# A feed-forward block on one core: another head and one more slot by seven products

## The chip, the core and the metric

The program runs on one core of one Trainium2 chip. TensorE (PE in the profile) does the matmuls, VectorE (DVE), ScalarE (ACT) and GpSimd (POOL) do the work on whole tiles, SyncE (SP) issues most of the DMAs. The metric is the device time of one execution in microseconds (us).

## What is computed

`x` is 4 batches of 1024 tokens of 512 numbers. The reference, cut to what matters:

```python
scale = cond @ norm_w.T + 1.0                       # (4, 512)
h = x * (scale[:, None, :] * rsqrt(mean(x * x) + EPS))
val, gate = split(h @ up_w.T, 2)                    # up_w: 4096 x 512
h = val * gelu(gate)                                # 2048 wide
hq = act_quant(h)                                   # 8 bit, one scale for each token
y = hq @ weight_quant(down_w).T + x                 # down_w: three values
```

## The kernel before, in words

The 2048 columns of `h` are made in 16 slots of 128 columns (`NJ`) for each batch, so there are 64 slots; slot g of batch 0 has the weights W_g, with 128 value rows and 128 gate rows. Each number of `x` and of W is split into two fp16 parts, high and low, and of the four products of parts three are taken, so a product of 128 x 256 by 256 x 512 is six matmuls (`TERMS`).

In batch 0 the slots below `SEVEN` are taken plainly: `plain_half(j, h)` runs 24 matmuls for each half of the tokens, 48 for a slot. From slot `SEVEN` on, and in all later batches, `slot(g)` takes seven products of sums and differences of blocks (A, B, E are its PSUM banks), 42 matmuls for a slot. What these seven products need of the weights is made by `s_sums`, `s_high`, `s_low` and stored with `s_spill`; what they need of `x` in batch 0 is made by the steps in `FIRST_T`. A slot at or above `SEVEN` gets its sums turned by one DMA transpose at once, and later batches load it as it is; one below has them turned at each later load (`s_load_x`, `s_load_y`).

The head is the part before the first product. SyncE loads `x` and W0 to W2. TensorE runs 23 idle matmuls (`keep_warm`), and among them the three small steps of the condition: `cond_first_row` (pc, line 685) spreads the condition's row over the partitions, VectorE forms the scale of batch 0 (`cond_scale`, `cond_largest`), TensorE turns the largest (line 715), VectorE makes a power of two of it (`cond_range`), TensorE spreads it (line 731). `first_sum` sums the squares of the first four tiles of `x`, `rsqrt` is an affine step and a power (POOL, lines 1001 and 1002) and gives `rs0`. `first_scale` multiplies each tile with its `rs0`, `first_turn` transposes the tile on TensorE. `w_range(j)` finds the largest of the weights' rows on VectorE (line 786) and their inverse `iv` (line 796); `w_scale(j)` multiplies them with it; `w_turn(j)` transposes them on TensorE (line 825); `w_high` and `w_low` copy the high part out of PSUM and subtract it for the low one (lines 850 to 862). `first_high` (ACT, line 1498) and `first_low` (DVE, line 1502) do the same for `x`. Then `plain_first` runs slot 0 for the first half of the tokens (24 matmuls, line 1199), in an order written by hand into which the turns of W1 and W2 are set.

Nothing of this is issued in the order of the code. All steps are recorded in a `Plan`; a planner places them by estimated durations and due times, `MENDS` is a list of random seeds by which it mends the waits that it foresees, `MOVES` is a list of pairs (step, step before which it is put), and what comes out is the order on each engine. Every engine then runs its own row in order and waits on semaphores.

Of the kernel before, what the change touches and what calls it, by code (L numbers as in the profile page):

```python
# [115 lines left out]
class Plan:  # L116
# [71 lines left out]

    def order(self):

        steps = self.steps
# [12 lines left out]
        self.lucks = [[(chance.random(), chance.random()) for _ in steps] for _ in range(MISSES)]  # L204
        for n in range(ROUNDS):
            margin, guard, chained, crowded = MARGINS[n % len(MARGINS)]
            self.needed(clock, chained)
            if crowded:
                self.crowd()
            for s in steps:  # L210
                s.margin, s.guard = margin, guard
            order, kept = self.placed()
            clock = self.replay(order)
        for n in MENDS:
            order, kept = self.mend(order, kept, random.Random(n))
        return self.moved(order)

    def moved(self, order):
# [12 lines left out]
        self.replay([s for row in rows.values() for s in row])  # L231
        return sorted(self.steps, key=lambda s: (s.start, s.n))

    def placed(self):
# [5 lines left out]
    def mend(self, order, kept, chance):  # L240
# [5 lines left out]
        for s in order:  # L246
            if s.eng == "PE":
                if s.start - last > 0.08:
                    waits.append((s.start - last, s))
                last = s.end  # L250
        s = chance.choices([s for _, s in waits], [w for w, _ in waits])[0]
        chain, swap, q = [], None, s.behind
        while q is not None and q.eng != "PE" and len(chain) < 20:
            chain.append(q)
            p = q.queue or q.behind
            if p is not None and p.n not in q.deps and chance.random() < 0.5:
                swap = chance.random() < 0.6 and p.eng != "PE" and p.late < q.late
                break
            q = p
        if swap:  # L260
            p.late, q.late = q.late + 2e-3, p.late - 2e-3
        elif chance.random() < 0.3 or not chain:
            t, late = s.start, [s.late for s in steps]
            self.needed(clock, chance.random() < 0.5)
            margin, guard, _, _ = chance.choice(MARGINS)
            for s, old in zip(steps, late):
                if s.tied or not t - 50.0 < s.late < t + 5.0:
                    s.late = old
                    continue
                s.margin, s.guard = margin, guard  # L270
                if s.eng != "PE":
                    s.late -= chance.random() ** 4
        else:
            sooner = 0.2 + 8.0 * chance.random() ** 2
# [77 lines left out]
    def replay(self, order, luck=None):  # L352
# [9 lines left out]
        while True:  # L362
# [19 lines left out]
            s, t = first[1], first[2]  # L382
            cost = s.alone
            if luck and s.eng != "PE":
                cost *= 0.96 + 0.12 * luck[s.n][0]
            if s.port:
                if port > t + 0.1:
                    s.behind = holder
# [4 lines left out]
            if s.wait:  # L393
                x, s.queue = t + ISSUE, None
                if s.wait > 0.1:
                    if dma > x:
                        x, s.queue = dma, last
                    dma, last = x + s.wait, s
                s.end = x + s.wait + LANDING + (luck[s.n][1] if luck else 0.0)
            if s.end > latest:  # L400
                latest = s.end

# [11 lines left out]
)  # L414
CROWD, ROOM = (45.0, 215.0), 1.05
MOVES = (
# [7 lines left out]
)  # L424
ROUNDS = 1
MENDS = (
# [7 lines left out]
)  # L434
MISSES, ISSUE, LANDING, RELOAD, FETCH, FERRY = 6, 1.2, 1.5, 6.5, 8.6, 4.0


# [113 lines left out]
def glu_quant_kernel(  # L551
# [246 lines left out]
    def w_range(j, t0=0, t1=2):  # L798
        w_factor(j, w_largest(j, t0, t1), t0, t1)
# [5 lines left out]

    ROWS = 3

    SEVEN = 9

    def w_scale(j, ts=(1, 0), eng=None):  # L810
        eng = eng or (ACT if j >= 5 else POOL)
# [684 lines left out]
    def first_high(h, k, pt):  # L1496
        c = slice(h * TOK, (h + 1) * TOK)
        ACT.activation(XP[:, 0, k, c], pt, AF.Copy, scale=scT[:, k, 0:1])

    def first_low(h, k, pt, eng=DVE):  # L1500
        c = slice(h * TOK, (h + 1) * TOK)
# [29 lines left out]
    first_sum(1)  # L1531
    first_sum(2)
    first_sum(3, DVE)
    w_range(0, 1, 2)
    rsqrt(ssq0[:, 0:4], rs0[:, 0:4])
    first_scale(2, DVE)
    first_scale(0, ACT)
    first_scale(1, POOL)
    first_scale(3, ACT)
    w_scale(0, (1,))  # L1540
    ptx = [po_bank(f"ptx_0_{k}") for k in range(3)] + [bank("A", 2, name="ptx_0_3")]
    for n in (2, 0, 1, 3):
        first_turn(n, ptx)
    book.tied = False
    w_turn(0, [bank("E", 2, name=f"pw_0_{t}") for t in (1, 0)], (1,))
# [560 lines left out]
```

## Time and profile before

| what | us |
|---|---|
| median of 3 runs (719.23 to 719.73) | 719.45 |
| the profiled execution | 719.23 |
| its span, from the first to the last instruction | 717.4 |
| TensorE busy in the span | 711.5 |
| VectorE / ScalarE / GpSimd busy | 605.2 / 409.8 / 130.0 |
| first matmul of slot 0 (line 1199) | 14.36 |
| first matmul of a slot by seven products (line 1141) | 112.20 |

The profiled execution's 719.23 is its span and 1.8 us around it. Times inside the program are counted from the start of the span. A line of the timeline has the start, the time taken, the engine, the line of the kernel, the operation, what it writes and reads with the shapes, how many instructions are merged in it, and in brackets the idle time of the engine before it with what ended it. TensorE's matmuls overlap in the records: one of 512 columns is shown with 0.38 us, but the next starts after 0.216.

### The profile page before, as it was taken

The page shows a single profiled execution, that of the slowest core. Times are in us where ns is not written, and L with a number is a line of the kernel's source. Part 1 is how long each engine was busy: PE and PEld are TensorE (multiplying, and loading weights), DVE is VectorE, ACT ScalarE, POOL GpSimd, SP SyncE. Part 2 cuts the span into 40 slices and gives each one's busy share as a digit, 9 for nine tenths or more (in the row PEclk, how much of TensorE's full clock was granted, in tenths as well). Part 3 has the DMA queues.
Part 4 walks back from the last instruction along what each step waited for, and adds up shares of the span by engine and source line. Part 5 has one row for each costly group of instructions (what it writes and reads, how often), then busy time and mean ns, then how long its engine had stood idle before and what let it go on. Part 6 is the DMA issues. An engine that isn't in the chain of part 4 may idle for free.

```text
span 717.4 us, 10113 instructions
## 1 busy us (share of the span) xinstructions
PE 711.5 (99%) x3625; PEld 355.8 (50%) x3625; DVE 605.2 (84%) x903; ACT 409.8 (57%) x671; POOL 130.0 (18%) x138
## 2 busy tenths in 40 slices
PE   8999999999999999999999999999999999999998
PEld 4544444444444456664444445665444444445744
DVE  7978998899899899878899887767878888956897
ACT  5677688784546897553435786533333775332454
POOL 4753141020100004660023003700011000000000
PEclk9999999999999999999999999999999999999999
DMA  7778999999785896759234555778233444453414
GB/s 261 253 205 208 240 227 252 194 257 268 219 227 133 210 245 173 223 153 211 67 101 110 118 129 142 176 191 173 73 118 103 102 102 99 99 98 104 150 57 146
DMA packets 189134, 118.74 MB, mean 166 GB/s; under 512 B 151302, under 2 KB 158359, under 8 KB 189084
## 3 DMA queue, kind: packets, MB, share of 16 engines
q1 hardware_dynamic: 188794, 117.77, 64.3%
q8 instruction: 28, 0.46, 0.3%
q10 hardware_dynamic: 290, 0.33, 0.1%
q14 instruction: 22, 0.18, 0.1%
HBM read 59.20 MB, written 23.09 MB: 115 GB/s over the span
## 4 chain that ended last, share of the span: by engine, by line
PE 97%; DMA 1%; ACT 1%; POOL 0%; DVE 0%; issue 0%; SPq 0%; POOLq 0%
PE A L1141 40%; PE E L1141 20%; PE B L1141 10%; PE po L1413 9%; PE E L1156 6%; PE A L1156 4%; PE B L1156 3%; PE po L1362 2%; PE E L1362 1%; PE A L1362 1%; DMA H<-in_x_dram 1%; PE B L1413 1%; PE B L1362 0%; PE A L1199 0%; PE po L1494 0%; PE po L825 0%
## 5 line engine op out<-in xcount | busy, mean ns | idle before, releaser
L1141 PEld LDWEIGHTS <-SXY 128*128 128x128 f16 x2184 | 213.7, 98 | 250.9
L1141 PE MATMUL A<-R,SXY 128*128 128x512 f16 x1188 | 276.3, 379 | 0.0
L1141 PE MATMUL E<-R,SXY 128*128 128x512 f16 x594 | 145.3, 379 | 0.0
L1334 DVE TENSOR_TENSOR H<-H,am 128x1024 f32<-128x1024 f32 x64 | 76.6, 1222 | 0.2
L1141 PE MATMUL B<-R,SXY 128*128 128x512 f16 x312 | 76.6, 379 | 0.0
L1275 DVE TENSOR_REDUCE gm<-H 128x512 f32<-128x1024 f32 x56 | 69.0, 1232 | 0.9
L1252 ACT ACTIVATE t<-t,sg 128x512 f32<-128x512 f32 x55 | 39.7, 721 | 51.0 <-DVE t L1249 51.0
L1239 DVE SCALAR_TENSOR_TENSOR H<-A,sg,t 128x512 f32<-128x512 f32 x55 | 41.2, 749 | 31.9 <-PE A L1141 31.6
L1291 POOL PARTITION_ALL_REDUCE am<-R x8 | 15.5, 1934 | 288.4 <-DVE R L1277 288.4
L1236 ACT ACTIVATE t<-B,sg 128x512 f32<-128x512 f32 x55 | 37.8, 687 | 42.7 <-PE B L1141 42.6
L1227 ACT COPY B<-A 128x512 f32<-128x512 f32 x55 | 31.4, 571 | 53.3 <-PE A L1141 53.1
L1249 DVE TENSOR_TENSOR t<-E,t 128x512 f32<-128x512 f32 x55 | 37.9, 689 | 28.2 <-PE E L1141 27.7
L1413 PE MATMUL po<-wd,R 128*128 128x256 fp8e4 (+1 forms) x448 | 57.0, 275 | 0.0
L1219 ACT COPY t<-A 128x512 f32<-128x512 f32 x55 | 32.2, 585 | 43.4 <-PE A L1141 39.0
L1255 DVE TENSOR_TENSOR v<-A,v 128x512 f32<-128x512 f32 x55 | 37.9, 690 | 20.4 <-PE A L1141 19.6
L1413 PEld LDWEIGHTS <-R 128*128 128x128 bf16 (+1 forms) x480 | 47.0, 98 | 13.1
L1231 ACT COPY v<-E 128x512 f32<-128x512 f32 x55 | 32.2, 586 | 31.9 <-PE E L1141 15.6
L1342 ACT ACTIVATE H<-H 128x1024 f32<-128x1024 f32 x38 | 39.7, 1049 | 8.5 <-DVE H L1334 8.3
L1258 DVE SCALAR_TENSOR_TENSOR H<-v,sg,t 128x512 f32<-128x512 f32 x55 | 41.7, 759 | 1.7 <-ACT t L1252 1.4
L1156 PEld LDWEIGHTS <-SXY 128*128 128x128 f16 x264 | 25.8, 98 | 30.5
L1346 ACT ACTIVATE R<-H 128x1024 bf16<-128x1024 f32 x38 | 39.6, 1052 | 1.0 <-DVE H L1086 0.5
L1277 DVE TENSOR_TENSOR R<-R,gm 128x512 f32<-128x512 f32 x56 | 38.4, 686 | 0.9
(270 smaller groups left out, 919.2 us busy)
## 6 DMA issues: line engine op xcount, KB each, us to landing
SXY<-s_dram SPq DMA_DIRECT2D x57, 256.0 KB, 2.7
H<-in_L_cond_up_w_dram SPq DMA_DIRECT2D x13, 512.0 KB, 4.1
SXY<-s_dram SPq DMA_DIRECT2D x15, 384.0 KB, 3.7
xr<-in_x_dram SPq DMA_DIRECT2D x19, 256.0 KB, 2.9
out_dram<-xr SPq DMA_DIRECT2D x19, 256.0 KB, 2.1
s_dram<-SXY SPq DMA_DIRECT2D x12, 384.0 KB, 3.6
s_dram<-SXY SPq DMA_DIRECT2D x5, 896.0 KB, 6.7
H<-in_x_dram SPq DMA_DIRECT2D x8, 512.0 KB, 4.8
```

The source lines that it names most:

```text
L1141: PE.matmul(o, s[:, w, k, :], xs(l, k), start=start and n == 0, stop=stop and n == len(TERMS) - 1, skip_group_check=True,)
L1156: PE.matmul(ps, a[k // 2][:, w, k % 2, :], XP[:, l, k, h * TOK : (h + 1) * TOK], start=n == 0, stop=n == len(terms) - 1,)
L1239: DVE.scalar_tensor_tensor(h_half(g - 1, 0), prev["A"], gain(g - 1, 0), prev["t1"], ALU.mult, ALU.mult)
L1249: DVE.tensor_tensor(prev["t2"], prev["E"], prev["t2"], ALU.add)
L1252: ACT.activation(prev["t2"], prev["t2"], AF.Gelu, scale=gain(g - 1, 1))
L1258: DVE.scalar_tensor_tensor(h_half(g - 1, 1), prev["v"], gain(g - 1, 0), prev["t2"], ALU.mult, ALU.mult)
L1275: DVE.tensor_reduce(gm[0], v, AX.X, ALU.max, apply_absolute_value=True)
L1277: return [largest, lambda: DVE.tensor_tensor(m, m, gm[0], ALU.max)]
L1334: DVE.tensor_tensor(v, v, r.to_broadcast([P, 2, TOK]), ALU.mult)
L1342: ACT.activation(v, v, AF.Copy, bias=MAGIC)
L1346: ACT.activation(q, by_tile(v), AF.Copy, bias=-MAGIC)
L1413: PE.matmul(po, w[:, j], m, start=start and j == 0, stop=stop and j == n - 1, skip_group_check=True,)
```

## The change

What the code does now, in the head and in slot 8:

```diff
-    SEVEN = 9
+    SEVEN = 8
...
     first_sum(3, DVE)
+    rsqrt(ssq0[:, 0:4], rs0[:, 0:4], DVE)
     w_range(0, 1, 2)
-    rsqrt(ssq0[:, 0:4], rs0[:, 0:4])
+    w_scale(0, (1,), ACT)
+    first_scale(0, DVE)
     first_scale(2, DVE)
-    first_scale(0, ACT)
-    first_scale(1, POOL)
-    first_scale(3, ACT)
-    w_scale(0, (1,))
+    first_scale(1, ACT)
+    first_scale(3, DVE)
...
-    for n in (2, 0, 1, 3):
+    for n in (0, 2, 1, 3):
         first_turn(n, ptx)
```

The affine step of `rsqrt` goes from GpSimd to VectorE (the power stays on GpSimd), three tiles of `x` are scaled on VectorE and one on ScalarE, and the gate rows of W0 on ScalarE in place of GpSimd. Slot 8 is taken by seven products. `first_high` gets an engine argument, which no call uses; `begin` does nothing with the empty `HEAD`.

The planner's tables are all new, so that the order on every engine differs from before in many places. `MOVES` has 288 pairs in place of 46, `MENDS` 68 other seeds, `mend` looks only at the first `REACH` matmuls (160, 400, 800 or 4000 of them in turn):

```diff
-    (1063, 1016), (56, 76), (96, 132), (2119, 2167), (98, 94), (1064, 1016), (307, 275), (295, 31),
+    (5604, 5615), (5603, 5614), (5602, 5611), (5601, 5602), (5598, 5601), (5608, 5596), (3183,
...
+        for s in [s for s in order if s.eng == "PE"][:reach]:
+            if s.start - last > 0.08:
+                waits.append((s.start - last, s))
+            last = s.end
```

Three places of the new order are shown, by the rows of one engine. Line numbers of the kernel after the change are 52 to 55 higher here: 1565 is 1510 (the idle matmuls), 737 is 685 (pc), 767 is 715, 877 is 825 (turns of weights), 1251 is 1199 (slot 0).

The first place is TensorE's row from its beginning, before the change: pc is its fourth matmul, behind three idle ones.

```order
L1510 LDWEIGHTS H
L1510 MATMUL A_89<-H 128x512
L685 MATMUL B_90<-H,one 128x128
L1510 LDWEIGHTS H
L1510 MATMUL A_91<-H 128x512
```

After the change the same stretch reads as follows, and ahead of it stand nine more idle matmuls.

```order
L1565 LDWEIGHTS H
L1565 MATMUL A_91<-H 128x512
L737 MATMUL B_90<-H,one 128x128
L767 MATMUL A_89<-ident,mx_92 1x128
L1565 LDWEIGHTS H
```

So pc is now TensorE's eleventh matmul, behind ten idle ones, and the turn of the largest follows it directly.

The second place is VectorE's row from the condition's power of two on (d, dg), before: `ux`, `dx`, the sum of squares of tile 3, the largest of W0's gate rows, one tile scaled, then the inverses and W0's turned gate rows (CAST).

```order
L725 TENSOR_SCALAR dg_94<-ident,d_0_93 1x1
L735 RECIPROCAL ux<-B_90 128x1
L738 COPY dx<-B_90 128x1
L1482 SCALAR_TENSOR_TENSOR R,ssq_0_87<-H 128x512
L786 TENSOR_REDUCE wam_95<-H 128x1
L659 TENSOR_SCALAR wam_95<-wam_95 128x1
L793 TENSOR_SCALAR sw<-wam_95 128x1
L1489 TENSOR_SCALAR H<-H,rs_0_88 128x512
L796 RECIPROCAL iv_96<-sw 128x1
L786 TENSOR_REDUCE wam_102<-H 128x1
```

After, from the sum of squares on, the rows to the CAST are these.

```order
L1541 TENSOR_SCALAR H<-H,rs_0_88 128x512 x3
L845 TENSOR_SCALAR sw<-wam_95 128x1
L838 TENSOR_REDUCE wam_102<-H 128x1
L848 RECIPROCAL iv_96<-sw 128x1
L711 TENSOR_SCALAR wam_102<-wam_102 128x1
L845 TENSOR_SCALAR sw<-wam_102 128x1
L789 TENSOR_SCALAR scT<-scT,ux 128x4
L848 RECIPROCAL iv_96<-sw 128x1
L838 TENSOR_REDUCE wam_95<-H 128x2
L711 TENSOR_SCALAR wam_95<-wam_95 128x2
L902 CAST SXY<-E_100 128x2x256
```

Ahead of these stand `dg`, the sum of squares, `dx`, the affine step on `ssq`, `ux` and the largest of W0's gate rows, in this order. The three scalings now stand ahead of both inverses of W0 (`iv`), and the largest of both halves of W1 (128x2) ahead of the CAST.

The third place is GpSimd's row and TensorE's at the turns of W1. GpSimd's row after the change, from the power on: the scaling of W0's value rows, the four sums of slot 0 (lines 919 to 922), the scaling of W1's value rows (`iv_103`).

```order
L1054 TENSOR_TENSOR rs_0_88<-ssq_0_87,neghalf 128x4
L869 TENSOR_SCALAR H<-H,iv_96 128x512
L919 TENSOR_TENSOR H<-H 128x256
L921 TENSOR_TENSOR H<-H 128x256
L922 TENSOR_TENSOR H<-H 128x256
L920 TENSOR_TENSOR H<-H 128x256
L869 TENSOR_SCALAR H<-H,iv_103 128x512
```

Before, the sums of slot 0 stood ahead of that scaling too, and the low parts of three of them (line 884) as well. TensorE's row before, where slot 0's first 17 matmuls end and W1 is turned (gate rows into po_97, value rows into po_98):

```order
L1199 LDWEIGHTS SXY
L1199 MATMUL A_89<-R,SXY 128x512
L825 MATMUL po_97<-ident,H 128x128 x4
L825 MATMUL po_98<-ident,H 128x128 x4
L1199 LDWEIGHTS SXY
```

After, the turn of W1's value rows stands here:

```order
L877 MATMUL E_101<-ident,H 128x128 x4
L1251 LDWEIGHTS SXY
L1251 MATMUL B_90<-R,SXY 128x512
L1251 LDWEIGHTS SXY
L1251 MATMUL A_89<-R,SXY 128x512
L1251 LDWEIGHTS SXY
L1251 MATMUL A_89<-R,SXY 128x512
L1251 LDWEIGHTS SXY
L1251 MATMUL B_90<-R,SXY 128x512
L877 MATMUL po_98<-ident,H 128x128 x4
```

So four matmuls of slot 0 stand ahead of it in place of 17. All 24 transposes of the first four tiles of `x` and of W0 stand ahead of slot 0 in both.

More of the change, by code (lines that the diff above doesn't have):

```diff
@@ L189, in order @@
     def order(self):
+        self.begin(HEAD)
         steps = self.steps
@@ L214, in order @@
         for n in MENDS:
-            order, kept = self.mend(order, kept, random.Random(n))
+            order, kept = self.mend(order, kept, random.Random(n), REACH[n % len(REACH)])
         return self.moved(order)
@@ L232, in moved, with begin @@
         return sorted(self.steps, key=lambda s: (s.start, s.n))
+    def begin(self, head):
+        if not head:
+            return
+        first, last, new = set(head), {}, {}
+        self.steps = [self.steps[n] for n in head] + [s for s in self.steps if s.n not in first]
+        for n, s in enumerate(self.steps):
+            new[s.n], s.n = n, n
+        for s in self.steps:
+            s.deps = {new[d] for d in s.deps}
+        for s in self.steps[: len(head)]:
+            if s.wait:
+                continue
+            if s.eng in last:
+                s.deps.add(last[s.eng])
+            last[s.eng], s.tied = s.n, True
     def placed(self):
@@ L238, in placed, with mend @@
         return sorted(self.steps, key=lambda s: (s.start, s.n)), kept
-    def mend(self, order, kept, chance):
+    def mend(self, order, kept, chance, reach):
         steps, last, waits = self.steps, 0.0, []
@@ L245, in mend @@
         clock = self.replay(order, chance.choice(self.lucks))
[L246 to L250, printed above, removed]
+        for s in [s for s in order if s.eng == "PE"][:reach]:
+            if s.start - last > 0.08:
+                waits.append((s.start - last, s))
+            last = s.end
         s = chance.choices([s for _, s in waits], [w for w, _ in waits])[0]
@@ L384, in replay @@
             if luck and s.eng != "PE":
-                cost *= 0.96 + 0.12 * luck[s.n][0]
+                cost *= 0.97 + 0.09 * luck[s.n][0]
             if s.port:
@@ L398, in replay @@
                     dma, last = x + s.wait, s
-                s.end = x + s.wait + LANDING + (luck[s.n][1] if luck else 0.0)
+                s.end = x + s.wait + LANDING + (0.7 * luck[s.n][1] if luck else 0.0)
             if s.end > latest:
@@ L426 @@
 MENDS = (
[7 rows of a table removed]
-)
[9 rows of a table added]
+)
+REACH = (160, 400, 800, 4000)
+HEAD = ()
 MISSES, ISSUE, LANDING, RELOAD, FETCH, FERRY = 6, 1.2, 1.5, 6.5, 8.6, 4.0
@@ L1494, in first_turn, with first_high @@
             PE.transpose(pts[k][:, c : c + P], X0[:, n, k * P : (k + 1) * P], ident)
-    def first_high(h, k, pt):
+    def first_high(h, k, pt, eng=ACT):
         c = slice(h * TOK, (h + 1) * TOK)
-        ACT.activation(XP[:, 0, k, c], pt, AF.Copy, scale=scT[:, k, 0:1])
+        if eng is ACT:
+            ACT.activation(XP[:, 0, k, c], pt, AF.Copy, scale=scT[:, k, 0:1])
+        else:
+            eng.tensor_scalar(XP[:, 0, k, c], pt, scT[:, k, 0:1], None, ALU.mult)
     def first_low(h, k, pt, eng=DVE):
```

59 rows, old and new, of tables (MENDS, MOVES) are left out of this document.

## The prediction

> **What bounds the kernel now.** I read the page first (busy times), then the busy times by stage, then the chain that ended last, then the first 45 us row by row. On the page TensorE is busy for nearly the whole span.
>
> ```profile
> span 717.4 us, 10113 instructions
> PE 711.5 (99%) x3625; PEld 355.8 (50%) x3625; DVE 605.2 (84%) x903; ACT 409.8 (57%) x671; POOL 130.0 (18%) x138
> ```
>
> The table by stage says where the rest is (columns: stretch, its length, busy time and instructions of PE, PEld, DVE, ACT, POOL, clock, DMA share, GB/s). From 20 us on PE is busy all the time, at the full granted clock; VectorE is at 9.97 of 10 in one stage, and the DMA engines are full around 100 us.
>
> ```profile
> 30.00:40.00 10.00, 10.00 (x56) 5.38 (x54) 9.97 (x19) 6.24 (x13) 6.66 (x9) 1.00 0.80 266
> 100.00:125.00 25.00, 25.00 (x118) 11.33 (x116) 22.07 (x43) 22.68 (x40) 3.56 (x4) 1.00 1.06 251
> 250.00:700.00 450.00, 450.00 (x2386) 233.26 (x2384) 370.48 (x482) 232.33 (x369) 71.17 (x73) 1.00 0.53 133
> ```
>
> The chain that ended last gives the price of a matmul and the start of slot 9.
>
> ```profile
> 39.43 2.59 PE A L1156 x12
> 112.36 3.45 PE A L1141 x16
> ```
>
> Twelve take 2.59 us, so one is 0.216. TensorE never catches up after 20 us: a microsecond that its products start later is a microsecond of the end, and a matmul less is 0.216 less. So the sum is short: matmuls removed, and the shift of the moment from which TensorE runs through.
>
> **Slot 8.** 48 matmuls become 42: 6 x 0.216 = **1.30 us less**. What it costs stands beside TensorE: three more copies on ScalarE and two more additions on VectorE, priced by the rows of the later slots (0.57 and 0.69 us), one more DMA transpose at once and six fewer in later batches.
>
> ```profile
> L1227 ACT COPY B<-A 128x512 f32<-128x512 f32 x55 | 31.4, 571 | 53.3 <-PE A L1141 53.1
> L1249 DVE TENSOR_TENSOR t<-E,t 128x512 f32<-128x512 f32 x55 | 37.9, 689 | 28.2 <-PE E L1141 27.7
> ```
>
> That is 1.7 us of ScalarE and 1.4 of VectorE in a stage in which each has 2 to 3 us idle of 25. I cost them at nothing; the cover is that idle time. If it is gone, each piece that is late costs its own length, 0.6 to 1.2 us. More delicate is that the sums of `x` and the turned weights are due 10.4 us sooner, at 102 us in place of 112; that is a rival below.
>
> **The condition behind ten idle matmuls.** These rows carry the head up to the power.
>
> ```profile
> 0.93 0.27 DVE L605 MEMSET H<- 128x256 uint32 x1
> 1.26 1.46 PE L1510 MATMUL A<-H 128*128 128x512 f16 x3 [1.26 <-DVE H L607]
> 2.65 0.79 PE L685 MATMUL B<-H,one 1*128 1x128 f32 x2
> 3.37 2.31 PE L1510 MATMUL A<-H 128*128 128x512 f16 x5
> 3.59 0.29 DVE L690 SCALAR_TENSOR_TENSOR R<-R,B 128x128 f32<-128x128 f32 x1
> 5.12 0.16 DVE L708 TENSOR_REDUCE mx<-scT 128x1 f32<-128x4 f32 x1
> 5.48 0.42 PE L715 MATMUL A<-ident,mx 128*1 128x128 f32 x1
> 5.94 0.28 DVE L721 TENSOR_REDUCE d<-A 1x1 f32<-1x128 f32 x1 [0.66 <-PE A L715]
> 6.60 0.20 DVE L725 TENSOR_SCALAR dg<-ident,d 1x1 f32<-1x1 f32 x1
> 7.17 2.98 PE L1510 MATMUL A<-H 128*128 128x512 f16 x13
> 7.76 0.69 DVE L1482 SCALAR_TENSOR_TENSOR R<-H 128x512 f32<-128x512 f32 x1 [0.26 <-DMA H<-in_x_dram]
> 8.37 0.08 DVE L1482 DVE_READ_ACCUMULATOR R<-H 128x1 f32 x1
> 9.04 1.06 POOL L1002 TENSOR_TENSOR rs<-ssq,neghalf 128x4 f32<-128x4 f32 x1
> ```
>
> The five idle matmuls from 3.37 reach to 5.48: 0.42 each, half the later pace. The warming memset now comes first on VectorE, where three short memsets stood ahead of it, so TensorE starts some 0.1 sooner, at 1.1. Ten at 0.42 put pc at 5.3, where it stood at 2.65. VectorE starts 0.94 after pc, at 6.25 if pc runs at the slow pace throughout, at 5.9 if the pace doubles under it; I take 6.1, since the slow pace is seen until 5.48. To the end of `mx` 1.69 pass (3.59 to 5.28), to line 721 another 0.66, of which some 0.2 was a wait behind idle matmuls, to the end of `dg` 0.86 (5.94 to 6.80). So `dg` ends at 6.1 + 1.69 + 0.5 + 0.86 = 9.15. The sum of squares of tile 3 stands behind it on VectorE: 9.1 in place of 7.76, where the DMA was last. It and its read take 0.69, to 9.8; `dx` and the affine step some 0.25; the step to GpSimd 0.1, the power 1.06: `rs0` at 11.15, the first scaling at **11.2** in place of 10.14. Bounds: 10.7 (faster idle matmuls, no waits between) and 11.5 (slow pace to the end of pc, 0.66 kept).
>
> The Trainium skill, "TensorE: Matmul & The Clock Gate", section "What's actually happening", says that the array runs at half its clock until one busy window of about 3.4 us, and that the window runs free of the kernel's start. The trace agrees (0.42 before 5.48, 0.216 later); by the earliest window, 4.5 us as an estimate of that page, pc would come 0.4 us sooner and the sum 0.4 lower.
>
> **From the scalings to the turn of W1.** Let T be the first scaling on VectorE. Before:
>
> ```profile
> 10.14 0.49 DVE L1489 TENSOR_SCALAR H<-H,rs 128x512 f32<-128x512 f32 x1 [0.66 <-POOL rs L1002]
> 10.54 0.16 DVE L796 RECIPROCAL iv<-sw 128x1 f32<-128x1 f32 x1
> 10.61 0.67 DVE L786 TENSOR_REDUCE wam<-H 128x1 f32<-128x512 f32 x1
> 11.31 0.15 DVE L659 TENSOR_SCALAR wam<-wam 128x1 int32<-128x1 int32 x1
> 11.79 0.15 DVE L796 RECIPROCAL iv<-sw 128x1 f32<-128x1 f32 x1
> 12.03 0.70 POOL L817 TENSOR_SCALAR H<-H,iv 128x512 f32<-128x512 f32 x1 [0.17 <-DVE iv L796]
> 12.81 0.73 POOL L867 TENSOR_TENSOR H<-H 128x256 f32<-128x256 f32 x1
> 13.50 0.73 POOL L868 TENSOR_TENSOR H<-H 128x256 f32<-128x256 f32 x1
> 14.19 0.72 POOL L869 TENSOR_TENSOR H<-H 128x256 f32<-128x256 f32 x1
> 14.36 2.10 PE L1199 MATMUL B<-R,SXY 128*128 128x512 f16 x9 [0.37 <-ACT R L1498]
> 14.99 0.73 POOL L870 TENSOR_TENSOR H<-H 128x256 f32<-128x256 f32 x1
> 16.52 1.90 PE L1199 MATMUL A<-R,SXY 128*128 128x512 f16 x8
> 17.89 0.70 POOL L817 TENSOR_SCALAR H<-H,iv 128x512 f32<-128x512 f32 x1
> 18.25 1.04 PE L825 MATMUL po<-ident,H 128*128 128x128 f32 x8
> 24.18 0.14 PEld L825 LDWEIGHTS po<-ident,H 128*128 128x128 f32 x1 [0.22 <-ACT R L852]
> ```
>
> A scaling is followed by the next instruction after 0.40, so three take 1.2; an inverse and the steps around the second largest take what they took (0.07, 0.67, then 0.2, 0.2, 0.2 to the last inverse): W0's second inverse ends at T + 2.6, where it was T + 1.8. GpSimd then scales W0's value rows (T + 2.7), makes four sums, each 0.80 after one that it needs and 0.69 after one that it doesn't (12.03, 12.81, 13.50, 14.19, 14.99), and scales W1's value rows from T + 6.45 to T + 7.15. TensorE's turn of them waits for that: **T + 7.2 = 18.4**. VectorE's inverse for W1 (T + 5.4) and the emptied bank are earlier, so GpSimd's row is last. ScalarE's new table load isn't: the load and the dummy Gelu behind it lie between its scaling of tile 1 (0.67) and W0's gate rows, which wait for the inverse at T + 2.0; 0.67 + 1.28 + 0.20 is T + 2.15, 0.15 late, and what follows it on VectorE has 0.3 to spare.
>
> ```profile
> 1.28 1.28 ACT L1461 ACT_TABLE_LOAD   x1 [1.28 <-PEq L2092]
> 10.13 1.34 ACT L1487 ACTIVATE H<-H,rs 128x512 f32<-128x512 f32 x2 [1.66 <-POOL rs L1002]
> ```
>
> The turn itself stood at about 18.7 before, so its time hardly moves. But 17 matmuls and four transposes lay ahead of it then, and four matmuls now. Put as the moment from which TensorE would run through: before, 14.36 and two waits (16.52 - 14.36 - 9 x 0.216 = 0.22, and 0.2 at 24.18), 14.75; after, 18.4 - 4 x 0.216 = 17.55. **2.8 us later.** After that turn I find no long wait: what the next matmuls read from VectorE comes 0.2 to 1 us ahead of them.
>
> **Sum.** The profiled execution's 719.23 (span 717.4 and 1.8 around it) - 1.30 + 2.8 = 720.7. The median of the runs, 719.45, is 0.2 above that execution, so I predict **721.0**, 1.5 us or 0.2% above before. T's bounds give +1.0 to +1.8; a wait more of 0.2 to 1 us, where VectorE has so little to spare, would come on top.
>
> **The rivals.**
>
> *The head is less late.* If TensorE's pace doubles by 4.5 us and GpSimd's instructions follow each other in 0.69 throughout, T is 10.6, the turn comes at T + 6.9 = 17.5, and the sum is +0.6: 720.0, not slower by what can be told. It decides at T + the GpSimd row = 18.3. For it: the slow pace is known from one execution. Against it: the pace was 0.42 to 5.48.
>
> *The turn of W1 isn't what TensorE waits for.* If GpSimd's row runs ahead of the condition, only the removed matmuls count: 719.45 - 1.3 = 718.1. Against it: the scaling needs an inverse that stands behind the scalings by `rs0`.
>
> *The idle matmuls lose their pace again.* From 5.3 to 9.2 TensorE now has only pc, a turn and three idle matmuls. If it falls back to 0.42, the ten idle ones last from 9.6 to 13.8, the 24 transposes at double length to 19, the CAST and W1's inverse come 3 us later, and the turn at about 20.7: 723.3. Against it: in the quoted row of 7.17, behind half a microsecond without work, thirteen take 2.98, 0.23 each. The same page of the Trainium skill has the array fall back after one idle window of 3.4 us; no row here shows it.
>
> *Slot 8's inputs come late.* It starts 10.4 us before slot 9 did, in a stage with the DMA engines full (1.06). A sum or a turned weight that is late holds TensorE for 1 to 2 us: 722 to 723. Against it: nothing waited there before, and VectorE has 3 us of 25 to give.
>
> *The change doesn't do what it says:* not here; the new order has 42 matmuls in slot 8.
>
> **How the numbers follow.** Forecast 0.55 (of it 0.20 within 0.2% and 0.35 above), head less late 0.17, cold idle matmuls or late inputs of slot 8 0.22, only the removed matmuls 0.06. The measurement tells apart about 0.2% (1.4 us). Faster 0.06, same 0.37, slower 0.57. The range leaves out the faster case and the far end of the late ones: 719.8 to 723.2.
>
> **What would show it.** In the profile after: pc (line 737) at 5.0 to 5.4; the sum of squares of tile 3 (line 1534 on VectorE) at about 9; `rs0` used at 11.2; GpSimd's scaling of W1 ending at 18.3; TensorE idle for 1 to 1.5 us ahead of the turn into `po` (line 877), and hardly any wait later; line 1193 with 42 more matmuls than line 1141. I am wrong if line 1251 runs through from 15 us, or if TensorE shows waits behind 30 us.

## The result, and the profile after

The changed kernel takes **722.33 us** (median of 4 runs, 722.21 to 724.04) where the kernel before took 719.45 (719.23 to 719.73). The ratio is 1.0044 with a 95% interval of 1.0032 to 1.0056: slower by 2.3 to 4.0 us. The prediction was 721.0, with a range of 719.8 to 723.2 and "slower" as the likeliest side. Its direction and its main mechanism held; two terms of its sum were too small, and one was missing. The profiled execution of after took 722.36 us, 3.13 more than that of before, and is typical of its runs.

The page's first lines show that TensorE works 0.3 us less than before, though the span is 3.1 us longer. What was lost is idle time.

```profile
span 720.6 us, 10080 instructions
PE 711.2 (99%) x3619; PEld 355.7 (49%) x3619; DVE 616.2 (86%) x908; ACT 412.0 (57%) x674; POOL 132.7 (18%) x134
```

Where it lies is read from the table by stage (columns as in the prediction). First four stages of before, then the same four of after.

```profile
0.00:12.00 12.00, 9.61 (x36) 4.04 (x37) 8.29 (x46) 4.88 (x10) 3.10 (x8) 1.00 0.72 228
12.00:20.00 8.00, 7.58 (x47) 4.67 (x48) 6.84 (x14) 6.34 (x15) 7.18 (x9) 1.00 0.97 338
40.00:50.00 10.00, 10.00 (x48) 4.51 (x46) 7.37 (x20) 7.83 (x16) 6.84 (x9) 1.00 0.80 187
700.00:717.40 17.40, 14.32 (x83) 7.82 (x80) 13.56 (x19) 7.07 (x7) 0.00 (x0) 1.00 0.41 151
```

```profile
0.00:12.00 12.00, 8.68 (x25) 3.27 (x26) 6.77 (x41) 3.88 (x8) 1.25 (x5) 0.86 0.79 254
12.00:20.00 8.00, 6.04 (x42) 4.17 (x41) 7.93 (x20) 7.00 (x14) 5.68 (x8) 1.00 0.65 243
40.00:50.00 10.00, 9.73 (x47) 4.38 (x46) 9.39 (x21) 7.24 (x16) 2.46 (x5) 1.00 0.74 209
700.00:720.60 20.60, 16.73 (x94) 8.93 (x92) 14.60 (x21) 8.08 (x8) 0.00 (x0) 1.00 0.36 130
```

Three things stand there. From 12 to 20 us TensorE is idle 1.96 us of 8, where it was idle 0.42. Between 40 and 50 it is idle 0.27. And in the last stage it is idle 3.87 us (20.60 less 16.73) in place of 3.08: the end behind the last matmul has grown. In the first 12 us it is idle 3.32 us in place of 2.39, but there it has only idle matmuls and the small steps of the condition. Beside these stands the granted clock, 0.86 in the first 12 us where it was 1.00. From 60 to 700 us TensorE is busy for all of the 640 us in both kernels; slot 8 has no waits.

The head of after, row by row, answers to the rows that the prediction showed of before. Line 737 is the condition's matmul (685 before), 767 and 783 are the two small steps behind it (715 and 731), 1565 the idle matmuls (1510), 1534 the sum of squares of tile 3 (1482), 1541 the scalings of x.

```profile
1.17 4.04 PE L1565 MATMUL A<-H 128*128 128x512 f16 x10 [1.17 <-DVE H L659]
5.14 0.48 PE L737 MATMUL B<-H,one 1*128 1x128 f32 x2
5.66 0.29 DVE L742 SCALAR_TENSOR_TENSOR R<-R,B 128x128 f32<-128x128 f32 x1 [2.15 <-PE B L737]
7.40 0.27 PE L767 MATMUL A<-ident,mx 128*1 128x128 f32 x1 [1.78 <-DVE mx L760]
8.04 1.43 PE L1565 MATMUL A<-H 128*128 128x512 f16 x3 [0.37 <-DVE d L773]
8.37 0.20 DVE L777 TENSOR_SCALAR dg<-ident,d 1x1 f32<-1x1 f32 x1
8.50 0.67 DVE L1534 SCALAR_TENSOR_TENSOR R<-H 128x512 f32<-128x512 f32 x1
9.40 0.58 PE L783 MATMUL B<-dg,one 1*128 1x1 f32 x2
9.92 3.09 PE L1565 MATMUL A<-H 128*128 128x512 f16 x10
10.02 0.16 DVE L790 COPY dx<-B 128x1 f32<-128x1 f32 x1 [0.84 <-PE B L783]
10.10 0.17 DVE L1053 TENSOR_SCALAR ssq<-ssq 128x4 f32<-128x4 f32 x1
11.46 1.28 DVE L1541 TENSOR_SCALAR H<-H,rs 128x512 f32<-128x512 f32 x3 [0.35 <-POOL rs L1054]
```

The first scaling stands at 11.46, where it stood at 10.14. Between 8.04 and 11.5 the idle matmuls are 0.43 apart again (three take 1.43), although line 767 had already run in 0.27; `dg` is ready at 8.57, but line 783 stands behind the three slow ones until 9.40. VectorE has `dx` ahead of the affine step and waits 0.84 us for it.

From there to the turn of W1 the rows answer to the second long fence of the prediction.

```profile
14.09 0.71 POOL L869 TENSOR_SCALAR H<-H,iv 128x512 f32<-128x512 f32 x1 [2.65 <-DVE iv L848]
16.28 0.39 PE L1251 MATMUL B<-R,SXY 128*128 128x512 f16 x1 [0.65 <-DVE SXY L902]
17.87 0.70 POOL L869 TENSOR_SCALAR H<-H,iv 128x512 f32<-128x512 f32 x1
18.19 0.68 DVE L911 TENSOR_TENSOR SXY<-E,SXY 128x512 f16<-128x512 f32 x1
18.62 0.66 PE L877 MATMUL po<-ident,H 128*128 128x128 f32 x4 [1.31 <-POOL H L869]
28.29 0.33 PE L877 MATMUL po<-ident,H 128*128 128x128 f32 x1
48.12 0.81 PE L1208 MATMUL E<-R,SXY 128*128 128x512 f16 x3 [0.27 <-DVE H L1236]
```

The turn waits for GpSimd's scaling, which ends at 18.57, with four products ahead of it, and stands 7.16 us behind the first scaling. Two waits follow that the prediction did not have, 0.20 us at 28.29 and 0.43 at 48.12, measured from where the matmul ahead would have released TensorE.

The end. From the start of VectorE's last instruction (these rows, before and after) the span lasts another 3.08 us in before and 3.80 in after.

```profile
714.36 0.48 DVE L1371 SCALAR_TENSOR_TENSOR R<-po,dq,R 128x256 f32<-128x256 f32 x1 [0.17 <-PE po L1362]
```

```profile
716.77 0.48 DVE L1423 SCALAR_TENSOR_TENSOR R<-po,dq,R 128x256 f32<-128x256 f32 x1 [0.39 <-PE po L1414]
```

The last output's transfer is issued 0.5 behind that row in both. Two things come later in after. SyncE goes through its closing waits in a fixed order. In before four of the five are past when the last transfer lands, in after the first of the five is the one for that transfer, and the other four follow it. GpSimd's next-to-last drain comes another 0.3 later and takes longer. The times below are us behind the start of VectorE's last instruction, as the trace has them.

```
                           before   after
last output packet ends      1.90    1.90
SyncE, first closing wait    0.23    2.30
SyncE, fifth closing wait    2.26    2.55
GpSimd, drain                2.59    3.16 (0.08 and 0.22 long)
end of the span              3.08    3.80
```

### The profile page after: what moved, and what is told of

Same layout as the page of the kernel before. It is cut to its first block, busy times and chain, and to the rows that moved or that the text cites. A ratio compares the mean times of both kernels' runs of the same rounds, so it can differ in the third digit from the quotient of the medians.

```text
span 720.6 us, 10080 instructions
## 1 busy us (share of the span) xinstructions
PE 711.2 (99%) x3619; PEld 355.7 (49%) x3619; DVE 616.2 (86%) x908; ACT 412.0 (57%) x674; POOL 132.7 (18%) x134
## 4 chain that ended last, share of the span: by engine, by line
PE 97%; DVE 1%; POOL 1%; issue 0%; POOLq 0%
PE A L1193 40%; PE E L1193 20%; PE B L1193 10%; PE po L1465 9%; PE E L1208 5%; PE A L1208 3%; PE B L1208 2%; PE po L1414 2%; PE E L1414 1%; PE A L1414 1%; PE A L1565 1%; PE B L1465 0%; PE B L1414 0%; PE po L877 0%; PE A L1251 0%; PE B L1251 0%
## 5 line engine op out<-in xcount | busy, mean ns | idle before, releaser
L1386 DVE TENSOR_TENSOR H<-H,am 128x1024 f32<-128x1024 f32 x64 | 79.0, 1260 | 0.2
L1310 DVE SCALAR_TENSOR_TENSOR H<-v,sg,t 128x512 f32<-128x512 f32 x56 | 44.0, 785 | 2.0 <-ACT t L1304 1.8
```

What stands on the lines that cost most here:

```text
L1310: DVE.scalar_tensor_tensor(h_half(g - 1, 1), prev["v"], gain(g - 1, 0), prev["t2"], ALU.mult, ALU.mult)
L1386: DVE.tensor_tensor(v, v, r.to_broadcast([P, 2, TOK]), ALU.mult)
```

## The experiments

All are measured against runs of the kernel before on the same chip (medians 719.62 to 719.68). A change of the order is a pair added at the end of `MOVES` (the step, and the step ahead of which it goes); that adds a line, so line 737 reads 738 there, and so on. For the others the rows of all engines are written out, from the order that the two kernels have, with the edits named. For each execution I took the first scaling on VectorE, called T, and the start of the last matmul from the trace:

```
               T      last matmul   behind T   last VectorE start to end
before       10.14      714.04       703.91      3.08
after        11.46      716.46       705.00      3.80
slot8_clean  10.30      712.92       702.62      3.35
head_alone   11.46      717.72       706.26      3.10
cond_early   10.69      715.66       704.97      3.81
cond_late    12.56      717.59       705.03      3.09
fill_after   11.36      716.34       704.98      3.81
fill_late    11.14      715.04       703.90      3.08
scale_ahead  12.29      717.52       705.23      3.81
table_early   9.88      714.85       704.97      3.79
pool_shift   13.00      718.47       705.48      3.36
scale_pool   10.42      717.17       706.76      3.39
```

The third column hardly depends on what happens ahead of T: with the rows of after behind T it is 704.97 to 705.00 four times, at T from 9.88 to 11.46. The last two rows are exceptions: there the granted clock is 0.50 for a while behind T (from 11.70 to 18.52 in pool_shift, from 17.92 to 21.33 in scale_pool), and the column is 0.5 and 1.8 higher. So the change splits into T, what lies between T and the last matmul, and the end.

**slot8_alone, slot8_smooth, slot8_clean: slot 8 without the head.** All three:

```diff
-    SEVEN = 9
+    SEVEN = 8
...
-        for n, before in MOVES:
...
+        for eng, row in ROWS.items():
+            rows[eng] = [self.steps[n] for n in row]
```

> Slot 8 by seven products without the new head: the kernel before with 42 matmuls in slot 8; what begins in its first 60 us stands in the order of before, the rest in the order of after. Theory (six matmuls less at 0.216, nothing behind them waits): 719.45 - 1.30 = 718.1, the last matmul 1.3 us earlier than before (712.7), and the 3.04 us from the start of the last VectorE instruction to the end of the span unchanged. Rival 1 (the 0.7 us that after has more behind its last matmul come with the new slot 8): 718.8. Rival 2 (slot 8's inputs come late, 10 us sooner): 719.5 or more, with PE waits between 85 and 115 us.

It took 724.78 us (ratio 1.0077, 1.0064 to 1.0090). Neither theory nor rival: the joint at 60 us held one matmul.

```profile
68.04 4.26 PE L1156 MATMUL E<-R,SXY 128*128 128x512 f16 x12 [4.24 <-DVE H L1184]
72.13 2.75 PE L1156 MATMUL A<-R,SXY 128*128 128x512 f16 x12
```

The bank's reader on VectorE stood behind steps of the other order. The twelve matmuls behind the pause take 4.26 where others take 2.75: 1.5 us more, lost to the pace. Taking off this pause (4.40, counted from where the matmul ahead would have released TensorE), a wait of 0.24 at 61.03, the 1.50 and the 0.40 by which T was later leaves the last matmul at 712.79, as the theory had it, but that is a subtraction and no measurement.

> The kernel before with 42 matmuls in slot 8 once more, with another joint: what begins in its first 50 us stands in the order of before, the rest in the order of after, and the rows of the other engines were evened out around the joint, so that no matmul is held there as it was in slot8_alone (4.4 us at 68). Theory (slot 8 by seven products is worth its six matmuls, and the loss of the change sits in the head): last matmul at 714.05 - 1.30 = 712.75; with 0.3 more behind it than before (as in slot8_alone): 718.4, 1.0 to 1.3 less than before. Rival (slot 8's inputs come too late once the joint is gone): PE waits between 85 and 115 us, total 719.5 or more.

720.12 us (ratio 1.0002, 0.9993 to 1.0011). The joint was smooth, but the evening out had moved steps in the head as well. This is the group of waits in which they show:

```profile
PE A L1199 <- DVE SXY L861: 1.0, 1, 1.0
```

So it says nothing clean of slot 8 either.

> The kernel before with 42 matmuls in slot 8, third joint: what begins in the first 38 us stands exactly as in before (in slot8_smooth the evening out had also touched the head, where TensorE then waited 1.0 and 0.3 us at 18 to 20 us), the rest in the order of after, evened out from 38 us on. Theory (slot 8 alone is a gain of its six matmuls; the loss is in the head): the last matmul 702.7 to 703.1 behind the first scaling on VectorE (before: 714.05 - 10.14 = 703.9, less 1.30, and up to 0.4 for a wait that the joint leaves near 60 us); with 0.27 more behind the last matmul, 718.4 to 718.9. Rival (the six matmuls don't come back because slot 8 waits elsewhere): 703.9 behind the first scaling, 719.7 or more.

**718.52 us** (ratio 0.9985, 0.9976 to 0.9993), faster than both kernels. This is its first scaling:

```profile
10.30 0.48 DVE L1489 TENSOR_SCALAR H<-H,rs 128x512 f32<-128x512 f32 x1 [1.01 <-POOL rs L1002]
```

T is that of before within 0.2, and the last matmul stands 702.62 behind T, 1.29 less than before. Six matmuls at 0.216 are 1.30. Slot 8 gives back all that it removes, and its inputs, 10 us sooner, hold nothing.

**head_alone: the head without slot 8.**

```diff
-    SEVEN = 8
+    SEVEN = 9
```

(on after, with the rows written out).

> The new head without the shorter slot 8: the kernel after with its 48 matmuls in slot 8; what begins in its first 60 us stands in the order of after, the rest in the order of before. Theory (all that the change costs is lost in the head, and the longer end belongs to it too): 722.33 + 1.30 = 723.6. Rival (the 0.7 us behind the last matmul belong to the order of the rest): 722.9. In both the last matmul starts at 717.7, 3.7 us later than before.

723.72 us (ratio 1.0061, 1.0047 to 1.0074). The last matmul stands at 717.72, as both said, 1.26 behind that of after. The longer end is gone (3.10), which is the rival's side: it does not belong to the head. The median lies above the rival's 722.9 and near the theory's 723.6, since the five runs spread from 722.85 to 724.92; the profiled one took 722.92.

T is 11.46 as in after, but it came about in another way. The condition's matmul ran slower here, so `dg` was ready at 9.23 in place of 8.57; the three idle matmuls ahead of line 783 ran at the full pace, and VectorE waited 0.18 for `dx` in place of 0.84. That the two executions agree in T is chance.

**cond_early: the condition back ahead of seven idle matmuls**, on after.

```diff
 MOVES = (
...
+    (35, 34),
 )
```

> After, with the condition's matmul (line 737) moved back ahead of seven of the ten idle matmuls. Theory (the condition's place on TensorE sets the first scaling): line 737 at 2.6, first scaling on VectorE at 10.1 in place of 11.46, turn of W1 (line 877 into po) at 17.3 in place of 18.62, total -1.3: 721.0. Rival (the first scaling or the turn is held by the transfers of x or by VectorE's own row): under 0.3 less, 722.0 to 722.3. Beside it: TensorE has no long gap ahead of its idle matmuls at 8 to 11 us any more, so they should stand 0.22 apart in place of 0.43.

721.54 us (ratio 1.0026, 1.0016 to 1.0036), 0.8 less than after, in place of 1.3.

```profile
7.74 2.33 PE L1566 MATMUL A<-H 128*128 128x512 f16 x10
8.52 0.69 DVE L1535 SCALAR_TENSOR_TENSOR R<-H 128x512 f32<-128x512 f32 x1 [1.30 <-DMA H<-in_x_dram]
10.69 1.28 DVE L1542 TENSOR_SCALAR H<-H,rs 128x512 f32<-128x512 f32 x3 [0.35 <-POOL rs L1055]
17.83 0.66 PE L878 MATMUL po<-ident,H 128*128 128x128 f32 x4 [1.30 <-POOL H L870]
```

The condition's place does set T, the whole rest moves with it (turn of W1 at T + 7.14), and the idle matmuls keep their pace (ten in 2.33). But with the condition out of the way x's second transfer is last: the sum of squares waits 1.30 us for it and starts at 8.52. In other executions that transfer let it start at 7.21 to 8.14.

**cond_late: the condition behind ten idle matmuls**, on before.

```diff
+    (36, 35), (37, 35), (38, 35), (39, 35), (40, 35), (48, 35), (49, 35),
```

> Before, with the condition's matmul (line 685) moved behind seven more idle matmuls, so that ten stand ahead of it, as in after; nothing else. Theory: the first scaling goes from 10.14 to about 11.4, the first product from 14.36 to about 15.6, and the total up by 1.0 to 1.3: 720.5 to 720.8. Rival (the head has slack elsewhere): under 0.3 more, 719.5 to 719.7.

722.72 us (ratio 1.0041, 1.0029 to 1.0054): 3.0 more, over twice what I expected, from the condition's place alone.

```profile
5.64 0.79 PE L686 MATMUL B<-H,one 1*128 1x128 f32 x2
10.05 4.87 PE L1511 MATMUL A<-H 128*128 128x512 f16 x13
12.56 0.49 DVE L1490 TENSOR_SCALAR H<-H,rs 128x512 f32<-128x512 f32 x1 [0.60 <-POOL rs L1003]
```

The condition's matmul ran at the slow pace here, and T is 2.42 later. The thirteen idle matmuls behind the pause take 4.87 where they took 2.98; they last past T, hold the turns of x, and put the last matmul 705.03 behind T in place of 703.91. That is the way in which the prediction's third rival (idle matmuls that lose their pace) lets slow idle matmuls cost time, in a kernel where nothing hides it. But here the pace was not lost: TensorE's matmuls stood 0.43 apart from the first one to 13.9 us, and the full pace came only then.

**fill_late and fill_after: the same idle matmuls, spread over the pause.** In cond_late and in after, six of the thirteen stand ahead of the two small steps.

```diff
-    def keep_warm(n):
+    def keep_warm(n, po=None, m=0):
...
-            PE.matmul(pz, warm[:, :P], warm, start=True, stop=True)
+            PE.matmul(po if i < m else pz, warm[:, :P], warm, start=True, stop=True)
+        return pz
...
-    keep_warm(2)
+    p2 = keep_warm(2)
...
-    keep_warm(13)
+    keep_warm(13, p2, 6)
```

> The kernel of cond_late (before, with ten idle matmuls ahead of the condition) with its other thirteen spread: four ahead of line 715, two ahead of line 731, seven behind. Theory (of cond_late's 3.0 us the condition's place is 1.2, and the rest is the thirteen idle matmuls at 0.43 behind a gap): later idle matmuls 0.22 apart, first product at 15.6 in place of 17.91, total 720.8. Rival (no change of the pace): idle matmuls 0.43 apart, first product at 17 or later, total 722 or more.

720.99 us (ratio 1.0016, 1.0007 to 1.0025), near the theory's 720.8.

```profile
4.85 0.48 PE L685 MATMUL B<-H,one 1*128 1x128 f32 x2
8.64 1.69 PE L1510 MATMUL A<-H 128*128 128x512 f16 x7
```

Seven in 1.69 is the full pace, and the last matmul is 703.90 behind T, as in before. In this pair of executions the filled pause gave back the 1.13 of cond_late that lay behind T. Part of the difference is chance: up to the condition's matmul both lists are the same, yet it ran in 0.48 here and in 0.79 there. Not all of it is: the slowest of the eleven runs here (721.35) is faster than the fastest of the five of cond_late (722.27).

> After, with the same 23 idle matmuls spread otherwise: ten, the condition's matmul, four, its turn (line 767), two, line 783, seven. Theory (TensorE's pace falls back in the 1.9 us without work ahead of line 767, and the three slow idle matmuls hold line 783, its copy dx and so the affine step): with work in the gap the later idle matmuls stand 0.22 apart, line 783 comes at 8.7 in place of 9.40, the first scaling at 10.7 in place of 11.46, and the total is 0.7 less: 721.6. Rival (the pace follows the time since the start, not the gap): idle matmuls still 0.43 apart at 9 to 11 us, total within 0.3 of 722.3.

722.28 us (ratio 1.0038, 1.0024 to 1.0052): no change of the total, which is the rival's number, but not for its reason.

```profile
5.55 0.79 PE L737 MATMUL B<-H,one 1*128 1x128 f32 x2
9.34 0.38 PE L783 MATMUL B<-dg,one 1*128 1x1 f32 x2 [0.53 <-DVE dg L777]
9.65 1.68 PE L1565 MATMUL A<-H 128*128 128x512 f16 x7
```

The pace is kept (seven in 1.68), and line 783 no longer stands behind idle matmuls. But the condition's matmul ran slow in this execution, and `dg` was ready 0.72 later than in after. In scale_ahead below and in head_alone it ran slow as well, and there the pause is left empty. T is 12.29 in scale_ahead, where the full pace came only at 13.7 us, and 11.46 in head_alone, where it came at 6.1; here it is 11.36. So the empty pause cost 0.93 us of T in one of these executions and 0.10 in the other, where the idle matmuls ahead of line 783 still ran at the full pace. That the totals agree rests on how often each case comes up, which a handful of runs does not settle.

**scale_ahead: GpSimd's scaling ahead of the fourth sum**, on after.

```diff
+    (123, 237),
```

> After, with GpSimd's scaling of W1's value rows (line 869) ahead of the last of the four sums of W0 (line 920), 0.67 earlier. Theory (GpSimd's row alone holds the turn of W1): turn at 17.95 in place of 18.62, total 721.7. Rival (VectorE's subtraction at line 911 stands right behind it, ending at 18.87, and the next product needs it): turn at 17.95, but the product behind it only 0.4 sooner, total 721.9; or nothing at all, if the sums moved behind are missed later.

723.19 us (ratio 1.0044, 1.0032 to 1.0057), no gain.

```profile
18.98 0.66 PE L878 MATMUL po<-ident,H 128*128 128x128 f32 x4 [0.23 <-POOL H L870]
19.17 0.68 DVE L912 TENSOR_TENSOR SXY<-E,SXY 128x512 f16<-128x512 f32 x1
19.91 0.39 PE L1252 MATMUL B<-R,SXY 128*128 128x512 f16 x1
20.81 0.39 PE L1209 MATMUL E<-R,SXY 128*128 128x512 f16 x1 [0.30 <-ACT SXY L905]
```

Behind T the turn is 0.47 sooner (T + 6.69; in head_alone, whose idle matmuls last as long behind T, it is T + 7.15). Then a product waits 0.22 for VectorE's subtraction (line 912, ending at 19.85) and another 0.46 for ScalarE's copy (both counted from where the matmul ahead would have released TensorE), which stands behind the copy of a sum that came later. The last matmul is 0.23 further behind T than in after. The rival holds, in its second form: what VectorE and ScalarE owe TensorE behind the turn is then late, by 0.68 us together.

**table_early and scale_pool: ScalarE's table load, and who scales tile 0**, both on cond_early.

```diff
+    (35, 34), (20, 24),
```

> cond_early with the dummy Gelu (line 1513) ahead of ScalarE's first sum of squares, where before had it; so the new table load leaves the stretch behind the first scaling. Theory (the load is hidden: the next product waits for VectorE's copy at line 902, not for ScalarE): the first turn of W0 0.3 to 0.5 us sooner, but the last matmul still 705.0 behind the first scaling, 721.5. Rival (ScalarE's row holds the first product): 704.5 behind the first scaling, 721.0.

721.43 us (ratio 1.0032, 1.0022 to 1.0041). The last matmul is 704.97 behind T, the same as with the load in the head's middle: it is hidden, as the prediction had it. The first turn of W0 came only 0.09 sooner behind T than in cond_early (T + 2.81 in place of 2.90), not the 0.3 to 0.5 that I expected.

```diff
-    first_scale(0, DVE)
+    first_scale(0, POOL)
```

> cond_early with the scaling of x's tile 0 on GpSimd in place of VectorE, so that VectorE scales two tiles. Theory (VectorE's third scaling stands ahead of W0's inverse and so of GpSimd's row and the turn of W1): turn of W1 6.7 to 6.8 behind the first scaling in place of 7.15, last matmul 704.6 behind it, 721.1. Rival (GpSimd's 1 us for the tile holds TensorE's turns of x, which stand ahead of those of W0): last matmul 705.3 behind the first scaling, 721.8.

720.63 us (ratio 1.0018, 1.0008 to 1.0027), 0.9 less than cond_early, though the two intervals overlap. The profiled execution is no typical one (722.66): TensorE ran at half pace from 17.92 to 21.33, and the last matmul is 706.76 behind T. The turn of W1 stands at 17.59 with T at 10.42: T + 7.17, no sooner.

```profile
10.42 1.33 DVE L1541 TENSOR_SCALAR H<-H,rs 128x512 f32<-128x512 f32 x2 [0.79 <-POOL rs L1054]
10.49 0.98 POOL L1541 TENSOR_SCALAR H<-H,rs 128x512 f32<-128x512 f32 x1
```

VectorE's two scalings take 1.33 beside GpSimd's, as long as three alone (1.28 in cond_early): the second one took 0.93 in place of 0.48. So VectorE came no sooner to what stands behind them, and whether the third scaling sets the turn is not tested. Of the 0.9 the end is 0.42 (3.39 in place of 3.81); where the other half comes from this profile can't tell.

**pool_shift: twelve short memsets on GpSimd**, on cond_early.

```diff
+    pad = cpool.tile([P, 1], F32, name="pad")
+    for _ in range(12):
+        nc.gpsimd.memset(pad, 0.0)
     book.emit(book.order())
```

> cond_early with twelve memsets of one column on GpSimd at its start, where it is idle for 9 us; they only lengthen its list of instructions. Theory (in after and cond_early an 8 KB transfer of instructions falls into GpSimd's closing steps and holds them): that transfer moves away from the end, and from the start of VectorE's last instruction to the end of the span pass 3.35 us in place of 3.81; total 721.1. Rival (it has another cause): 3.81 stays, 721.5.

724.50 us (ratio 1.0072, 1.0056 to 1.0088). The end is 3.36, as the theory had it, and the transfer of instructions at the end is gone. But T is 2.3 us later than in cond_early, and with TensorE at half pace behind it another 0.5 went. The 2.3 us have a reason that I don't know: GpSimd's power starts 3.2 us after the affine step (8.52 to 8.69) that it needs, and no row shows what it waited for.

```profile
8.52 0.17 DVE L1054 TENSOR_SCALAR ssq<-ssq 128x4 f32<-128x4 f32 x1
11.91 1.05 POOL L1055 TENSOR_TENSOR rs<-ssq,neghalf 128x4 f32<-128x4 f32 x1 [9.37 <-issue]
```

## Why the prediction was right, and where it was short

Its sum was -1.30 + 2.8 for the profiled execution, +1.5; that execution came out at +3.13. The terms:

```
                                   forecast   measured
slot 8                              -1.30      -1.29
first scaling (T)                   +1.06      +1.32
T to the moment of running through  +1.74      +1.71
waits behind the turn of W1          0         +0.63
the end behind the last matmul       0         +0.72
```

(Slot 8 is measured in slot8_clean. T is 11.46 less 10.14. The moment is 18.62 less four matmuls, 17.76 or T + 6.30; in before it was 14.73 or T + 4.59, from 14.36 and two waits of 0.22 and 0.15.)

**Slot 8** was right to a hundredth, and so was its cover: the added copies and additions are hidden (slot8_clean).

**The condition behind ten idle matmuls** was the right cause, and cond_early shows it by undoing it. T was foreseen at 11.2 with an upper bound of 11.5 and came at 11.46, but by two errors that partly cancel. VectorE started on pc at 5.66, not 6.1, since the pace doubled just under it, and `dg` ended at 8.57, not 9.15. Then `dx` and the affine step, put at "some 0.25" behind the sum of squares, ended 1.1 behind it: 0.84 of that is VectorE's wait for line 783 behind three slow idle matmuls. It could have been read from the new order, in which `dx` stands ahead of the affine step and line 783 behind three idle matmuls; I had counted the length of `dx` and not its wait. How the two errors come out differs from one execution to the next, as head_alone shows.

**From T to the turn** was right: T + 7.2 foreseen, T + 7.16 measured, GpSimd's row last, four products ahead, 1.31 us of wait where I had said 1 to 1.5. What scale_ahead adds is that this wait is no lever by itself.

**"After that turn I find no long wait"** was the step that failed in size: 0.20 us at 28.29 and 0.43 at 48.12 came on top. I had allowed "a wait more of 0.2 to 1 us" in words and put nothing in the sum. The prediction had also named waits behind 30 us as a sign that it is wrong, and the one at 48.12 is such a wait: on this point it was. At 48.12 VectorE is the one that is late, in a stage where it is now busy 9.39 of 10 us; before it was 7.37.

**The end** was missing. I took the time from the last matmul to the end as fixed by the last output. It depends on the program too: 3.08 to 3.10 with the rows of before behind 60 us (before, head_alone, cond_late, fill_late), 3.35 with the new slot 8 in the three kernels on before, 3.79 to 3.81 in after and four of its variants. 0.27 of the 0.72 is the order of SyncE's closing waits, which the three kernels with 3.35 share with after. The other 0.45 goes with GpSimd's list of instructions: in five executions with 3.80 an 8 KB transfer of instructions falls at the very end (the row below is of the DMA queues of after from 715 us on: packets, MB, share), and with twelve memsets more, or one scaling more, on GpSimd it is gone and the end is 3.36 and 3.39. These five have 134 instructions on GpSimd; the nine other executions have 135 to 146, and in none of them does that transfer stand at the end.

```profile
q14 instruction: 1, 0.01, 0.5%
```

That transfer starts 0.05 to 0.2 us after the end of the span, so it isn't itself what GpSimd waited for. That the longer end goes with the length of the list is shown, how it does is open.

**The rivals.** Idle matmuls that lose their pace were given 723.3 and a row against them: the thirteen in 2.98 in before. They did lose it in after, for 3.4 us, but paid through line 783 and not through the turns of x, as most of the slow stretch lay ahead of T. The row quoted against it came from a list in which TensorE had been busy from 3.4 to 6.3 us; the change took just that away. Slot 8's inputs coming late is refuted by slot8_clean, and the head less late by T. What I did not try is the turn of W1 with its 17 products ahead restored in the new head, since products of the new order read what that turn writes.

## What to carry to other kernels

Split a small difference at a moment that everything behind depends on (here the first scaling): what stands behind it was the same to 0.03 us in four executions, and off by 0.5 and 1.8 in two in which TensorE fell to half pace behind it, while the totals of single runs of one kernel differed by up to 3.4 us. When a step moves back on an engine, look for each later instruction that is queued behind its results on the other engines, with its wait and not just its length. And a gain in the middle of a kernel (slot 8) is worth testing without its companions: alone it beat both kernels.

## What the runs showed of the hardware

**The array falls back to half pace after a pause, and takes its time to return.** In slot8_alone TensorE stood still for 4.2 us at 64 to 68; the next stretch then has a granted clock of 0.61, and twelve matmuls take 4.26 us in place of 2.75.

```profile
64.00:68.00 4.00, 0.00 (x0) 0.00 (x0) 3.39 (x7) 2.64 (x6) 0.67 (x2) 0.96 0.31 114
68.00:72.00 4.00, 3.96 (x12) 1.51 (x12) 3.84 (x7) 1.61 (x4) 2.07 (x2) 0.61 0.55 208
```

In after 1.8 us without work and a few short instructions around them were enough (three idle matmuls in 1.43 at 8.04): of the 3.41 us ahead of the fall, 4.67 to 8.08, TensorE was busy for 1.26. The trace's record of the clock changes in steps of 3.41 us. Counted from its first entry on, in all fourteen executions it falls at the end of every such stretch in which TensorE worked 1.38 us or less, and of none in which it worked 1.76 or more. When the pace doubles also changes from one execution to the next: with the same list of instructions the condition's matmul took 0.48 at 5.14 in after and 0.79 at 5.55 in fill_after and scale_ahead, which alone moves what follows by some 0.7 us. The Trainium skill, "TensorE: Matmul & The Clock Gate", section "What's actually happening", says both: the array is slow unless a window of about 3.4 us was busy, falls back after an idle one, and the window runs free, so that the moment differs between runs. The traces agree, but for the idle window: here one with 1.26 us of work was idle enough. The prediction wrote of the falling back that no row showed it; now rows do.

**The granted clock of the profile misses the first slow stretch.** In pool_shift it reads 1.00 for the first 6 us, while three idle matmuls take 1.46 there, and 0.50 at 12 to 16 us. The trace's record of the clock has its first entry at 4.87 us there (4.67 in after, 13.91 in cond_late), where the distance between the matmuls halves, and the table counts the time ahead of it as full.

```profile
0.00:6.00 6.00, 4.67 (x13) 1.73 (x14) 3.94 (x29) 1.28 (x1) 1.37 (x16) 1.00 0.64 220
12.00:16.00 4.00, 2.46 (x12) 2.46 (x13) 2.97 (x11) 2.82 (x4) 1.34 (x2) 0.50 1.01 376
```

At the start of a kernel the distance between matmuls is the better witness.

**The length of GpSimd's list of instructions can have a price**: 0.45 us at the end go with it in after. In pool_shift, with twelve memsets more, one instruction in the head starts 3.2 us late, for which the profile names nothing; whether the length is the cause there is open.
